# Decoder block on one core: three products in column quarters, the bias moved to the residual, two DMAs for four, and new places

## The chip, the cores and the metric

The kernel runs on one core of a Trainium2 chip. A core has five engines, each with an in-order queue: TensorE (PE; its weight loads are listed as PEld), VectorE (DVE), ScalarE (ACT), GpSimd (POOL) and SyncE (SP), which here issues nearly all DMA transfers. The metric is the device time of one execution in microseconds (us).

## The reference

For 128 sequences of 64 rows with 128 features (8192 rows) the reference computes three sublayers, each followed by a residual addition and a layer norm:

```python
x = _layernorm(x + _L0_attn_ref(x, ...))           # linear attention, 16 heads of 64, 32 exp features
x = _layernorm(x + _L0_xattn_ref(x, ctx_1024, ...))  # softmax attention, 16 heads of 8
x = _layernorm(x + _L0_ffn_ref(x, ...))            # ternary weights, 128 -> 512 -> 128, gelu, inner layer norm
```

The linear attention takes `q' = exp(q wq_feat)`, `k' = exp(k wk_feat)`, divides `q' (k'^T v)` by `q' . sum(k') + 1e-6`, and projects with `Wproj` plus a bias. The softmax attention scales scores by 1/sqrt(8). The feed-forward part replaces both weight matrices by signs, with zeros for small entries, takes the exact gelu, normalises the 512 hidden values of a row with weight and bias, and projects back. Everything is fp32.

## The kernel before

The rows are cut into 16 groups of 512 rows: 8 sequences, or four *row tiles* of 128 rows. For each group a fixed list of steps is made; a step is a Python closure that issues its instructions on several engines. Nothing is scheduled by a compiler: `PLACE` gives each step a number, group g adds `g * ROUND` (44) and a shift from `SHIFT` (one of three dictionaries, by the first letter of the step's name, indexed by group), one-time preparations have their numbers in `PREP`, all steps are sorted, and their instructions are issued in that order. So the order on each engine's queue is the order of these numbers. A step of the second and third sublayers is placed one round later than its group (`r = g + 1`), and its number may exceed 44 by much, so that in one round PE works on the linear attention of group g, the softmax attention of group g-1 and the feed-forward part of groups g-2 and g-3.

The steps of a group are these (t counts row tiles, b sequences, c blocks of 128 of the 512 features):

- `lx`, `lc`, `lg`: loads of x transposed, the context transposed, and x; `lxs`, `lgs`, `xs` split such a tile into an fp32r high part (ACT) and the rest (POOL or DVE). A product of two split operands is three fp32r matmuls (`product3`, L427 to L429).
- `K0-3`, `Q0-3`: projections to features and their exp on ACT (kp, qp). `ks`, `kT`: the sums of k'. `G0-3`: k'^T x by sequence, in the 64-row shape (L530), copied out to gT by DVE (0, 3) or ACT (1, 2). `D`, `dT`: the denominators and their reciprocals as a table dT, `E0-3`: their spread over features (L582), multiplied into qp on DVE. `M0-7`: gT times the folded matrix U by sequence (L596), copied out to m by ACT, two sequences at a time. `Y0-3`: the output, x1 = bias product (L610) + qp m (L615) + x, with statistics on DVE; `Yn`: the norm.
- `xk`, `xq`: the projections of the softmax attention, each cut into three bf16 pieces (`pieces`), which six DMAs each copy into interleaved rows of `krep` and `qrep`. `xv`: the values (L659), copied by ACT into the block tile vbd. `xt`: four transposes of x1 (L670). `X0-3`: scores once, only for their row maxima on DVE (L700). `xm`: the maxima transposed (L705), negated and written as two bf16 pieces, mn, which go by DMA into two spare rows of each half of `qrep` (L712). `S0-3`: scores again, now with the maxima subtracted, and exp to pt on ACT (L728). `P0-7`: pt times values (L744). `C0-1`: division and transposition on DVE. `O0-1`: the output projection (L771) plus xb (`xr`: x1 plus bias, on POOL), statistics; `xn`: the norm on ACT.
- `ft`: transposes of x2 (L792). `fb`: the bias added to x2 on POOL. `fw0-1`: the first product (L807, L808) and gelu on ACT to gf. `fs0-1`: squares of gf on ACT to sk, summed on POOL to sq. `fo0-1`: the last product (L833, 130 columns: 128 outputs, and two for the mean) and the mean of the squares (L834, one column). `fv`: mean and variance, rstd on POOL; `fx`: scale and residual, statistics, on DVE; `fn`: the norm on ACT and the DMA out.

PE's array is used in several shapes, given by `tile_position`. Full width is one 128x128 weight tile. In a *column quarter* the weights are 128x32, four such products stand side by side, and each writes 32 partitions of the result. ks, D, M, Y and P are quarters; G uses two halves of 64 rows; X and S use 64x64 quadrants; the rest is full width. An fp32 matmul is two instructions in the profile, an fp32r matmul one.

PSUM has two double banks (`two()`: G, fw, M, X, S) and four single banks (`one()`: all others). A buffer comes free when its reader has copied it out, so an engine that reads late keeps PE from starting a later step.

Of the kernel before, what the change touches and what calls it, by code (L numbers as in the profile page):

```python
# [55 lines left out]
)  # L56
BIG = 5
# [27 lines left out]
def decoder_block(  # L85
# [347 lines left out]
    def shift(g, place):  # L433
        return SHIFT[2 if place[0] == "f" else 1 if place[0] in "xXSPCO" else 0].get(g, 0)
# [191 lines left out]
    def pieces(step, ps, bias, roles, rep):  # L626
# [7 lines left out]
        for i, part in enumerate(roles):  # L634
            nc.sync.dma_start(out=rep[i::HD], in_=pc[:, part, :])
# [339 lines left out]
```

## Time and profile before

| | us |
|---|---|
| median of 3 runs (lowest to highest) | 739.92 (739.57 to 741.57) |
| the profiled execution's own time | 740.87 |
| its span, first to last instruction | 738.9 |
| PE busy | 687.4 |
| DVE busy | 572.9 |
| ACT busy | 504.3 |
| POOL busy | 323.4 |
| rstd of the four layer norms and the inner one on POOL (L385, 64 of them) | 66.0 |
| PE waiting for POOL's sum of squares (once) | 5.1 |
| PE waiting for DVE's copies of gT (12 times) | 4.3 |
| PE waiting for the DMA of the maxima (3 times) | 2.3 |

How to read it: a line of the timeline gives the start, the duration, the engine, the line of the program, the operation, what it writes and reads, and how many instructions were merged; in brackets stands the idle time just before, and what ended it. Matmuls overlap in the array, and their listed durations include the way through it; the cost of one inside a full stream is the distance between starts. The granted clock (PEclk) is the TensorE clock as a share of full speed.

### The profile page before, as it was taken

The page shows a single profiled execution, that of the slowest core. Times are in us where ns is not written, and L with a number is a line of the kernel's source. Part 1 is how long each engine was busy: PE and PEld are TensorE (multiplying, and loading weights), DVE is VectorE, ACT ScalarE, POOL GpSimd, SP SyncE. Part 2 cuts the span into 40 slices and gives each one's busy share as a digit, 9 for nine tenths or more (in the row PEclk, how much of TensorE's full clock was granted, in tenths as well). Part 3 has the DMA queues.
Part 4 walks back from the last instruction along what each step waited for, and adds up shares of the span by engine and source line. Part 5 has one row for each costly group of instructions (what it writes and reads, how often), then busy time and mean ns, then how long its engine had stood idle before and what let it go on. Part 6 is the DMA issues. An engine that isn't in the chain of part 4 may idle for free.

```text
span 738.9 us, 36655 instructions
## 1 busy us (share of the span) xinstructions
PE 687.4 (93%) x16551; PEld 576.9 (78%) x16551; DVE 572.9 (78%) x1379; ACT 504.3 (68%) x757; POOL 323.4 (44%) x383
## 2 busy tenths in 40 slices
PE   6989999999999999999999999999999999976753
PEld 5767878787878888887878788887888787865653
DVE  1568898797879797988879787979889796958532
ACT  2636565867688687877686886878686877654750
POOL 4744414263553626263634526262635445143451
PEclk9989999999999999999999999999999999996875
DMA  7005131302122131413032221314131312203000
GB/s 191 3 31 136 43 106 31 102 24 77 55 75 75 49 101 34 117 34 92 31 84 65 76 75 47 103 34 116 35 80 42 82 53 52 71 24 82 19 23 20
DMA packets 58428, 47.82 MB, mean 65 GB/s; under 512 B 7952, under 2 KB 54032, under 8 KB 58272
## 3 DMA queue, kind: packets, MB, share of 16 engines
q1 hardware_dynamic: 57632, 45.37, 22.6%
q8 instruction: 129, 2.11, 1.2%
q0 software_dynamic: 320, 0.08, 0.2%
q14 instruction: 27, 0.22, 0.1%
q10 hardware_dynamic: 320, 0.03, 0.0%
HBM read 15.58 MB, written 4.19 MB: 27 GB/s over the span
## 4 chain that ended last, share of the span: by engine, by line
PE 68%; DVE 18%; POOL 4%; ACT 4%; DMA 2%; issue 2%; SPq 1%; POOLq 0%; ACTq 0%; DVEq 0%
PE two L596 13%; PE one L833 8%; PE one L615 8%; PE one L427 6%; PE one L428 4%; PE one L429 4%; PE two L530 3%; DVE bns L390 3%; PE two L697 3%; POOL rstd L385 2%; PE one L517 2%; DVE x L851 2%; PE one L610 2%; DVE gT L395 2%; PE one L582 2%
## 5 line engine op out<-in xcount | busy, mean ns | idle before, releaser
L596 PE MATMUL two<-U,gT 128*32 128x128 f32 x4096 | 123.4, 275 | 0.8 <-DVE mx L700 0.5
L596 PEld LDWEIGHTS two<-U,gT 128*32 128x32 f32 x4096 | 112.0, 111 | 1.8 <-DVE mx L700 0.6
L397 ACT COPY m<-two 128x1024 f32<-128x1024 f32 x64 | 64.9, 1013 | 30.3 <-PE two L596 30.1
L399 POOL TENSOR_SCALAR khl<-kp 128x512 fp32r<-128x512 f32 x32 | 20.2, 631 | 137.6 <-ACT kp L496 137.6
L833 PE MATMUL one<-w2c,gf 128*128 128x130 f32 x512 | 78.1, 301 | 1.5 <-ACT gf L810 1.5
L700 DVE TENSOR_REDUCE mx<-two 128x16 f32<-128x1024 f32 x64 | 74.9, 1213 | 3.3 <-PE two L697 3.3
L833 PEld LDWEIGHTS one<-w2c,gf 128*128 128x128 f32 x512 | 71.4, 210 | 4.8 <-ACT gf L810 2.1
L410 POOL TENSOR_TENSOR sq<-sk 128x512 f32<-128x512 f32 x16 | 20.8, 1299 | 116.9 <-ACT sk L816 116.9
L385 POOL TENSOR_TENSOR rstd<-veps,mhalf 128x4 f32<-128x4 f32 x64 | 66.0, 1032 | 5.3
L615 PE MATMUL one<-m,qp 128*32 128x128 f32 x2048 | 68.1, 273 | 0.0
L383 POOL TENSOR_SCALAR veps<-mv 128x4 f32<-128x4 f32 x64 | 15.4, 240 | 116.2 <-DVE mv L844 73.8
L423 ACT ACTIVATE x<-x,nm,rstd 128x128 f32<-128x128 f32 x128 | 51.3, 482 | 20.6 <-DVE nm L422 20.6
L728 ACT ACTIVATE pt<-two 128x1024 f32<-128x1024 f32 x64 | 62.7, 1021 | 1.9 <-PE two L725 1.7
L390 DVE BATCH_NORM_STATS2 bns<-x 128x6 f32<-128x128 f32 x192 | 55.5, 289 | 5.5
L615 PEld LDWEIGHTS one<-m,qp 128*32 128x32 f32 x2048 | 57.4, 110 | 0.2 <-issue 0.2
L508 ACT ACTIVATE qp<-one,bqk 128x512 f32<-128x512 f32 x64 | 43.7, 684 | 16.3 <-PE one L429 12.0
L496 ACT ACTIVATE kp<-one 128x512 f32<-128x512 f32 x64 | 38.3, 598 | 22.0 <-PE one L429 13.5
L530 PE MATMUL two<-khl,xgh 64*128 64x512 f32 x256 | 49.0, 418 | 4.6 <-DVE gT L395 4.3
L707 ACT ACTIVATE mn<-one 64x128 bf16<-64x128 f32 x16 | 4.3, 270 | 70.1 <-PE one L705 70.1
L744 PE MATMUL one<-pt,vbd 128*32 128x64 f32 x2048 | 46.7, 224 | 0.5 <-DVE x L851 0.5
L410 POOL TENSOR_TENSOR sq<-sq,sk 128x512 f32<-128x512 f32 x32 | 40.9, 1280 | 6.1 <-ACT sk L816 4.8
L842 DVE COPY mv<-one 128x2 f32<-128x2 f32 x32 | 4.9, 154 | 49.4 <-PE one L834 49.4
(217 smaller groups left out, 1812.6 us busy)
## 6 DMA issues: line engine op xcount, KB each, us to landing
krep<-pc SPq DMA_DIRECT2D x96, 128.0 KB, 2.4
qrep<-pc SPq DMA_DIRECT2D x96, 128.0 KB, 3.0
xT<-in_x_T_dram SPq DMA_DIRECT2D x16, 256.0 KB, 3.1
xg<-in_x_dram SPq DMA_DIRECT2D x16, 256.0 KB, 3.1
cT<-in_ctx_T_dram SPq DMA_DIRECT2D x16, 256.0 KB, 3.3
out_dram<-x SPq DMA_DIRECT2D x16, 256.0 KB, 2.4
qrep<-mn SPq DMA_DIRECT2D x64, 8.0 KB, 1.8
wTk<-in_L_attn_Wk_T_dram SPq DMA_DIRECT2D x1, 512.0 KB, 4.4
```

The lines of the kernel that those rows point to most:

```text
L385: nc.gpsimd.tensor_tensor(r, v, mhalf, ALU.pow)
L390: nc.vector.bn_stats(s, src)
L397: nc.scalar.copy(dst, src)
L410: eng.tensor_tensor(dst, a, b, op)
L423: nc.scalar.activation(x[:, t, :], x[:, t, :], AF.Identity, scale=r[:, t : t + 1], bias=nm[:, t : t + 1])
L530: nc.tensor.matmul(gps[:, b, :], lhsT=xp[r, t, :], rhs=z.khl[t // 2][r, kp, t % 2, :], start=(i == 0), stop=(i == 2), tile_position=(64 * ...
L596: nc.tensor.matmul(z.mps[b // 2][32 * j : 32 * j + 32, b % 2, c * D : c * D + D], lhsT=z.gT[b // 4][:, b % 4, h * F : h * F + F], rhs=w.U[ ...
L615: nc.tensor.matmul(yps[32 * i : 32 * i + 32, 0:D], lhsT=z.qp[:, c, t * P + 32 * i : t * P + 32 * i + 32], rhs=z.m[q // 4][:, q % 4, c, :], ...
L700: nc.vector.tensor_reduce(z.mx[:, :, :, t], sps.rearrange("p h (c k) -> p h c k", k=S), AX.X, ALU.max)
L728: nc.scalar.activation(z.pt[t].rearrange("p h b c q -> p (h b c q)"), sps.rearrange("p h n -> p (h n)"), AF.Exp, scale=HD ** -0.5)
L744: nc.tensor.matmul(z.cps[i // 4][32 * c : 32 * c + 32].rearrange("p (n k q) -> p n k q", k=2, q=32)[:, q // 32 : q // 32 + 2, k, :], lhsT= ...
L833: nc.tensor.matmul(ps[:, o : o + WF], lhsT=z.gf[c // 2][:, c % 2, n], rhs=w.w2c[:, c, :], start=(c == 0), stop=(c == NFC - 1))
```

## The change

Seven things are changed; what is computed stays the same.

1. `Y`: the bias product is no longer the first of the matmuls that add up in a tile of Y. A new step `W` computes it for all four row tiles of the group into one bank, at full width and in fp32r, and DVE adds the bank to xg, the residual.
2. `O`: each of the four output products of a group (two in each of two steps) becomes four products with 32 columns of weights.
3. `xv`: so do the four products of the values.
4. `fo`: so do the sixteen products of the last feed-forward matrix, and the mean of squares. For the last group alone, the two tiles of squares get separate buffers, and PE adds up the four parts instead of POOL.
5. `xm`: the maxima go to `qrep` in two DMAs of 64 rows in place of four of 32.
6. `pieces`: the six DMAs go out sorted by piece.
7. `PREP`, `SHIFT` and `PLACE` get new numbers, so the order of steps changes everywhere.

```diff
 PREP = {
...
+    "lb": -167.2995, "lk": -149.8596, "lc2": -141.5964, "c1": -137.7757, "lq": -112.8302, "lv": -47.1274,
+    "fk": -39.9216, "x0": -37.5866, "c0": -32.4310, "wb": -31.6615, "fq": -25.4067, "bqk": -11.7754, "U0": -11.4537,
+    "c2": -9.5186, "U1": -6.7768, "x1": -3.4930, "WB": 6.0100, "E": 8.5443, "x2": 17.9416, "c3": 18.6377,
+    "end": 19.6009, "w0": 45.9851, "w1": 82.4437, "w2": 93.0686, "w3": 128.7876,
...
+        @at(g, "W")
+        def _():
+            ps = one()
+            for t in range(GT):
+                n = slice(t * P, t * P + P)
+                nc.tensor.matmul(ps[:, n], lhsT=z.dT[:, n], rhs=w.WB, start=True, stop=True)
+            nc.vector.tensor_tensor(z.xg.rearrange("p t d -> p (t d)"), ps, z.xg.rearrange("p t d -> p (t d)"), ALU.add)
...
             yps = one()
-            for i in range(4):
-                n = slice(t * P + 32 * i, t * P + 32 * i + 32)
-                nc.tensor.matmul(yps[32 * i : 32 * i + 32, 0:D], lhsT=z.dT[:, n].bitcast(FP), rhs=w.WB.bitcast(FP), start=True,
-                                 stop=False, tile_position=(0, 32 * i))
...
-        for i, part in enumerate(roles):
+        for part, i in sorted((part, i) for i, part in enumerate(roles)):
             nc.sync.dma_start(out=rep[i::HD], in_=pc[:, part, :])
...
             for i in range(2):
-                for h in range(2):
-                    o = 64 * h + R2 - 2 + i
-                    nc.sync.dma_start(out=qrep[o : o + 1], in_=mn[32 * h : 32 * h + 32, i, :])
+                nc.sync.dma_start(out=qrep[R2 - 2 + i :: R2], in_=mn[:, i, :])
...
             for i in range(2):
-                nc.tensor.matmul(ps[:, i * D : i * D + D], lhsT=z.cnT[k][:, i, :], rhs=w.cwo, start=True, stop=True)
+                for j in range(4):
+                    r = slice(32 * j, 32 * j + 32)
+                    nc.tensor.matmul(ps[r, i * D : i * D + D], lhsT=z.cnT[k][:, i, r], rhs=w.cwo, start=True, stop=True,
+                                     tile_position=(0, 32 * j))
...
-            s = later.f1.tile([P, 2, GN], FP, tag="sk", name="sk")
+            s = later.f1.tile([P, 2, GN], FP, tag="sk1" if k and g == NG - 1 else "sk", name="sk")
             nc.scalar.activation(s.rearrange("p i n -> p (i n)"), z.gf[k].rearrange("p i n -> p (i n)"), AF.Square)
-            if k == 0:
+            if g == NG - 1:
+                z.sk[k] = s
+            elif k == 0:
...
                 for c in range(NFC):
-                    nc.tensor.matmul(ps[:, o : o + WF], lhsT=z.gf[c // 2][:, c % 2, n], rhs=w.w2c[:, c, :], start=(c == 0), stop=(c == NFC - 1))
-                nc.tensor.matmul(ps[:, o + WF : o + WF + 1], lhsT=z.sq[:, n], rhs=rff, start=True, stop=True)
+                    for j in range(4):
+                        q = slice(32 * j, 32 * j + 32)
+                        nc.tensor.matmul(ps[q, o : o + WF], lhsT=z.gf[c // 2][:, c % 2, n][:, q], rhs=w.w2c[:, c, :],
+                                         start=(c == 0), stop=(c == NFC - 1), tile_position=(0, 32 * j))
+                for j in range(4):
+                    q = slice(32 * j, 32 * j + 32)
+                    sq = [z.sk[c // 2][:, c % 2, n] for c in range(NFC)] if g == NG - 1 else [z.sq[:, n]]
+                    for c, s in enumerate(sq):
+                        nc.tensor.matmul(ps[q, o + WF : o + WF + 1], lhsT=s[:, q], rhs=rff, start=(c == 0),
+                                         stop=(c == len(sq) - 1), tile_position=(0, 32 * j))
```

The tables of numbers are best read as the order that they give. One round in the middle, step and group, before:

```
K0.9 xq.7 fw0.5 D2.8 P5.6 M0.8 dT.8 P7.6 M1.8 M4.8 M5.8 fs0.5 M2.8 M3.8 C1.6 O0.6 fw1.5 E2.8 K1.9 E1.8 xv.7 lc.8
X0.7 X1.7 K2.9 E0.8 lx.10 ks0.9 xs.8 ks1.9 M6.8 M7.8 E3.8 K3.9 lgs.9 O1.6 X2.7 X3.7 Y0.8 Y2.8 ks2.9 Y1.8 fs1.5 Y3.8
ks3.9 xm.7 Q0.9 fn.4 Q1.9 xn.6 Q3.9 lg.10 fo0.5 kT.9 xr.7 S0.7 S1.7 Q2.9 Yn.8 fo1.5 fv.5 ft.6 lxs.10 fb.6
P0.7 P1.7 S2.7 P2.7 P3.7 S3.7 fx.5 xk.8 G0.9 G1.9 D0.9 D1.9 P4.7 D3.9 P6.7 C0.7 xt.8 G2.9 G3.9
```

and after:

```
K0.9 xv.7 fs1.5 M4.8 O0.6 M5.8 M2.8 O1.6 lx.10 M3.8 E0.8 K1.9 X0.7 X1.7 E3.8 lc.8 E1.8 K2.9 ks0.9 fn.4
M6.8 M7.8 ks1.9 X2.7 E2.8 K3.9 lg.9 W.8 X3.7 ks2.9 Y0.8 Y1.8 fb.5 Y2.8 Y3.8 ks3.9 xm.7 kT.9 xs.8 Q0.9 Q3.9 Q2.9
xn.6 fo0.5 S0.7 Yn.8 S1.7 fo1.5 fv.5 lgs.9 ft.6 S2.7 P0.7 fx.5 P2.7 P3.7 P1.7 S3.7 Q1.9 xk.8 G0.9 xt.8 G1.9
P4.7 xr.7 C0.7 D0.9 D3.9 lxs.10 G2.9 G3.9 xq.8 fw0.6 P5.7 P6.7 P7.7 fs0.6 C1.7 D2.9 D1.9 M0.9 M1.9 fw1.6 dT.9
```

The start before: `lk c0 lb lc2 fk bqk c1 lq lx.0 lg.0 lxs.0 fq K0.0 lv x0 K1.0 K2.0 lx.1 ks0.0 lgs.0 ks1.0 K3.0 U0 ks2.0 ks3.0 U1 Q0.0 Q1.0 Q3.0 lg.1 kT.0 x1 E Q2.0 lxs.1 G0.0 G1.0 D0.0 D1.0 D3.0 wb G2.0 G3.0 K0.1 c2 D2.0 M0.0 dT.0 M1.0 M4.0 x2 M5.0 M2.0 M3.0 WB E2.0`; after: `lb lk lc2 c1 lq lx.0 lv fk x0 lxs.0 c0 wb fq K0.0 lx.1 K1.0 K2.0 ks0.0 ks1.0 K3.0 lg.0 bqk ks2.0 U0 c2 ks3.0 kT.0 U1 Q0.0 Q3.0 Q2.0 x1 lgs.0 Q1.0 WB G0.0 G1.0 E D0.0 D3.0 lxs.1 G2.0 G3.0 D2.0 D1.0 M0.0 x2 M1.0 c3 dT.0 end K0.1 M4.0 M5.0 M2.0 lx.2 M3.0 E0.0`.

More of the change, by code (lines that the diff above doesn't have):

```diff
@@ L433, in shift @@
     def shift(g, place):
-        return SHIFT[2 if place[0] == "f" else 1 if place[0] in "xXSPCO" else 0].get(g, 0)
+        return SHIFT[2 if place[0] == "f" else 1 if place[0] in "xXSPCO" else 0].get(g, 0) + EDGE.get(g, {}).get(place, 0)
     def at(g, place):
@@ L658, in _ @@
             for t in range(GT):
-                nc.tensor.matmul(ps[:, t * P : t * P + P], lhsT=z.cT[:, t * P : t * P + P],
-                                 rhs=w.cwvT.rearrange("p o c h e -> p (o c h e)"), start=True, stop=True)
+                for j in range(4):
+                    r = slice(32 * j, 32 * j + 32)
+                    nc.tensor.matmul(ps[r, t * P : t * P + P], lhsT=z.cT[:, t * P : t * P + P][:, r],
+                                     rhs=w.cwvT.rearrange("p o c h e -> p (o c h e)"), start=True, stop=True,
+                                     tile_position=(0, 32 * j))
             v5 = ps.rearrange("p (t o n e) -> p t o n e", t=GT, o=2, e=HD)
@@ L832, in _ @@
                 for c in range(NFC):
[L833 to L834 removed]
+                    for j in range(4):
+                        q = slice(32 * j, 32 * j + 32)
+                        nc.tensor.matmul(ps[q, o : o + WF], lhsT=z.gf[c // 2][:, c % 2, n][:, q], rhs=w.w2c[:, c, :],
+                                         start=(c == 0), stop=(c == NFC - 1), tile_position=(0, 32 * j))
+                for j in range(4):
+                    q = slice(32 * j, 32 * j + 32)
[3 more added lines that the diff above has]
+                                         stop=(c == len(sq) - 1), tile_position=(0, 32 * j))
         @at(r, "fv")
@@ L920, in _ @@
                                 ALU.subtract)
-    groups = [SimpleNamespace(pt={}, kp={}, khl={}, cps={}, cnT={}, mps={}, gT={}, m={}, gf={}, fps={}) for _ in range(NG)]
+    groups = [SimpleNamespace(pt={}, kp={}, khl={}, cps={}, cnT={}, mps={}, gT={}, m={}, gf={}, sk={}, fps={}) for _ in range(NG)]
     for g in range(NG):
```

5 lines of the change are left out of this document (4 added, 1 removed), and 42 rows, old and new, of tables (PLACE, PREP, SHIFT).

## The prediction

> **What bounds the kernel now.** I read the page first (busy shares, then the slices), then the times by windows, the waits of TensorE (PE), and last the timeline of one middle round and of the end. Page and windows:
>
> ```profile
> PE 687.4 (93%) x16551; PEld 576.9 (78%) x16551; DVE 572.9 (78%) x1379; ACT 504.3 (68%) x757; POOL 323.4 (44%) x383
> ...
> PEclk9989999999999999999999999999999999996875
> ...
> 40.00:60.00 20.00, 17.31 (x286) 13.86 (x285) 12.55 (x30) 6.37 (x11) 7.53 (x10) 0.83 0.16 50
> 160.00:640.00 480.00, 474.61 (x11998) 400.41 (x11987) 404.28 (x979) 364.85 (x546) 218.69 (x233) 1.00 0.25 68
> ...
> 700.00:720.00 20.00, 12.02 (x64) 10.41 (x64) 8.99 (x34) 9.88 (x18) 11.30 (x12) 0.76 0.05 15
> 720.00:739.00 19.00, 6.84 (x32) 6.76 (x32) 4.08 (x19) 1.65 (x4) 2.54 (x5) 0.59 0.09 26
> ```
>
> Columns of a window: length, then busy time of PE, PEld, DVE, ACT, POOL; PEclk; DMA share; GB/s. The reader should see two regimes. From 160 to 640 us PE is busy 474.6 of 480 us at full clock: a round (one group of 512 rows) costs what PE's instruction stream costs, 40.8 us (the transposes of the maxima stand at 365.23, 406.07, 446.76, 487.55). Before 60 and after 640 us PE waits, and its clock drops to 0.83 and 0.59.
>
> Inside a busy PE the matmul durations overlap, so costs are read from start to start. The timeline of a middle round:
>
> ```profile
> 396.27 0.40 PE L582 MATMUL one<-dT,E 128*128 128x512 f32 x1
> 396.60 0.64 PE L517 MATMUL one<-kp,ksel 128*32 128x128 f32 x16
> ...
> 399.95 0.60 PE L771 MATMUL one<-cwo,cnT 128*128 128x128 f32 x4
> 400.48 0.71 PE L697 MATMUL two<-krep,qrep 62*64 62x64 bf16 x64
> 401.12 0.42 PE L610 MATMUL one<-WB,dT 128*32 128x128 f32 x8
> 401.37 1.06 PE L615 MATMUL one<-m,qp 128*32 128x128 f32 x32
> 402.24 0.40 PE L517 MATMUL one<-kp,ksel 128*32 128x128 f32 x8
> ...
> 407.61 1.06 PE L833 MATMUL one<-w2c,gf 128*128 128x130 f32 x8
> 408.50 0.28 PE L834 MATMUL one<-rff,sq 128*128 128x1 f32 x2
> ...
> 420.44 0.66 PE L670 MATMUL one<-ident,x 128*128 128x128 f32 x4
> 421.48 0.50 PE L530 MATMUL two<-khl,xgh 64*128 64x512 f32 x2 [0.38 <-DVE gT L395]
> ```
>
> Three readings. Quarter products cost (402.24-401.37)/32 = 27.2 ns each, 109 ns for the four of a full width; L833 at full width costs (408.50-407.61)/8 = 111 ns: **quarters alone save nothing**. A change of array shape costs: L582 takes 0.33 us ahead of a quarter step, 0.23 between its like, and the first full-width matmul after another shape takes 0.34. So about 0.10 us to leave a shape, another 0.11 to enter full width, 0.09 to enter the 64-row shape of G, 0.02 to enter the others. And the one regular wait is 0.38 us at the third G for a copy of gT.
>
> **The change part by part (steady round).**
> *Bias.* L610 goes: 0.24 + 3 x 0.22 = -0.90 us. W puts four 128-wide fp32r matmuls of 128 columns in its place. Nearest rows: transposes of the same shape, L670 and L792, 0.46 us for 4; below, L834 (same weights, one column) 70 ns, so 0.28; above, L427's 512 columns, 0.23 each, so 0.93. I take 0.46: size and type agree. W stands right behind K3, so it adds no change of shape. On DVE it adds one 128x512 add, 0.675 us (row L583). DVE is busy 404.3/480 x 40.8 = 34.4 us a round, so 35.1 after. Queued behind it are the maxima of X3 and the adds of Y. I lay the new order out with the costs above: Y0 wants the last product with E (E2) at 25.6 us after the round's xk, DVE, which does E2 ahead of W, gives it at 25.2. Hidden, with 0.4 to spare; without that cover it costs its 0.68.
> *Last feed-forward product.* A pair of row tiles now takes 2.15 us (407.61 to 409.76). In quarters: 2 x 32 x 27.2 ns x 130/128 = 1.77, and 2 x 8 one-column quarters at 13.8 ns (L744: 16 in 0.22) = 0.22: 1.99. Two pairs: -0.32. If a one-column quarter cost as much as a 128-column one (27.2), +0.11.
> [...]
> *Output.* L771: 4 in 0.36 us among full-width neighbours, twice; in quarters 16 x 27.2 = 0.435: +0.15. *Values.* L659: 0.99 less 0.10 for the change of shape, 0.89; in quarters 0.87: 0.
> *New places: shapes.* I sorted the steps of one round by their places and counted neighbours on PE of unlike shape: 22 before, 27 after, of which the two at xm's sides are alike in both. The others by kind: into full width 0.21 each, 7 and 8; into G 0.19, 2 and 3; the rest 0.12, 11 and 14. That is 3.17 and 3.93: +0.76. Each unquartered fp32 product also leaves its successor 0.09 slower (the L427 behind L834 takes 0.32); three such places vanish: -0.27.
> *New places: waits.* 0.37 at G2 and 0.15 between K0 and xq (424.00-423.62 is 0.38 for a 0.23 step) can go. In the new order G1 lies between the transposes and G2, so G2 has 0.3 us of slack; but G3 then waits for ACT's copy of G1, ready 0.15 ahead of it, and X1 for the copy of M2M3, ready about 0.2 late. I leave 0.25 of the 0.52: -0.27. SP: lx, lc, lg and the out-transfer keep one place each per round; sorting the parts of qrep puts three transfers ahead that need no later piece; between xq and X0 lie 12.3 us (before 11.5), against 0.7 + 6 x 0.78 + 3.0 us for the pieces. xr (1.28 us on POOL) now comes ahead of C0, 11 us before O0 reads it; fb (1.29, POOL) comes a round later than its ft, still 8 us before fx. xgl, behind rstd on POOL, is ready 0.8 us ahead of G0.
> *Round:* -0.90+0.46-0.32+0.15+0.76-0.27-0.27 = **-0.39**; bounds: no waits left and W at 0.28: -0.8; W at 0.93, one-column quarters at 27.2, waits as before: +0.8. Fourteen rounds: **-5.5** (-11 to +11).
>
> **Start.** Between 40 and 51 us PE waits 1.43 us (for dT, whose cast took 3.48 instead of 0.43 while POOL filled qrep), then 1.26 (nhalf of WB), and runs until 51 at half clock, where 64 quarters take 3.26 us instead of 1.86. The new order has WB and the memsets of wb and c2 long before; krep's cast (2.29) and qrep's memset (3.5) still precede dT. I expect E0 at 41.6 instead of 42.1 and no second wait: 0.5 + 1.3 + 1.2 of slow clock = **-3** (-5.5 if the clock stays up, 0 if dT is as late).
>
> **End.** Two DMAs of maxima for four: issuing four takes 2.8 us. In the middle they are hidden (4.6 us of PE work from xm to S0), worth nothing. At 653.9, where no later group fills the gap, PE waits 1.69 + 0.41 us for them; two issues of 0.70 less: **-1.4** (0 to -2). The last group's sum of squares:
>
> ```profile
> 714.30 0.71 PE L833 MATMUL one<-w2c,gf 128*128 128x130 f32 x4 [1.29 <-ACT gf L810]
> 720.08 0.59 PE L834 MATMUL one<-rff,sq 128*128 128x1 f32 x2 [5.07 <-POOL sq L410]
> 720.53 2.08 PE L833 MATMUL one<-w2c,gf 128*128 128x130 f32 x8
> ...
> 716.30 1.06 ACT L816 ACTIVATE sk<-gf 128x1024 f32<-128x1024 f32 x1 [2.05 <-POOL sq L410]
> 717.43 2.60 POOL L410 TENSOR_TENSOR sq<-sq,sk 128x512 f32<-128x512 f32 x2 [1.17 <-ACT sk L816]
> ```
>
> PE waits 5.07 us for squares that ACT could not start (their tile was still read by POOL) and POOL then summed, and goes on at half clock (1.87 us for 8 instead of 0.89), to 726.93. After the change the second square has its own tile: ready at 714.24 + 1.06 = 715.3, no POOL. PE goes on at 714.3 with half a row tile (0.44) and three whole ones (0.88 each, as above), and for each of the four tiles 32 one-column quarters, since the four parts are now summed on PE (32 x 13.8 ns = 0.44): 4.8 us at full clock, 9.7 at half, so it ends at 719.1 to 724.0. I take the middle, rounded: **-5** (-2.9 to -7.8). What is late next is the gelu, then fv and fx as before.
>
> *Sum:* -5.5-3-1.4-5 = -14.9 on the profiled execution's 740.87 (span 738.9 and 1.97 around it): 726.0. That execution lies 0.95 above the median of 739.92: **725**.
>
> **The rivals.** *ACT becomes the bound at X1 (slower).* From fw0 to M3 the new order gives ACT two table loads (1.28 each), two gelus (1.02), two squares (1.06), kp and khl (0.60, 0.59), four copies to vbd (1.58) and three of m (1.01) before X1's buffer is free: 12.5 us, about 11.8 from start to start (a copy of 1.01 is followed after 0.91, 430.28 to 431.19), against 11.9 of PE work, where before vbd and a square stood elsewhere. For: no margin. Against: ACT is busy 364.9 of 480 us. Every us late is paid in each of 14 rounds; with the rest as forecast, the result is slower beyond (14.9+2.2)/14 = 1.2 us a round; at 1.5 the time is 725 + 21 = 746. Chance 0.12.
> *The shapes eat it.* Waits stay at 0.52 or W costs 0.93: the round gains 0 and the ends give 9.4: 730.5. For: five more changes are certain. Band 730 to 737.7, chance 0.25.
> *All waits go:* -0.82 x 14, start -5.5, end -9.8: 713. Band below 720, chance 0.14.
> *The change does nothing that counts:* W at 0.93 and one-column quarters at 27.2 give +0.5 x 14 = +7, the ends 9: 738. Within 0.3% (2.2 us, what a measurement of this kernel can tell from nothing), chance 0.10.
> The forecast, 720 to 730: 0.39.
>
> **How the numbers follow.** Faster: 0.39 + 0.25 + 0.14 = 0.78; same 0.10; slower 0.12. Range 714 to 742: from the case with no waits to the edge of the slower case, leaving out that case and a little below. The forecast's own range is 720 to 730.
>
> **What would show it.** W's four matmuls at about 0.46 us from start to start; L610 gone; 27 changes of shape a round; period 40.4. The third G without its wait for gT. In the end no wait of PE for POOL's sq, and the last one-column products less than 10 us after the last gelu. In the start no wait behind WB. Wrong it would be with a period of 41 or more, and waits of X for ACT's copies of m, or of G for gT.

## The result and the profile after

The changed kernel takes 763.29 us (median of 4 executions, 759.06 to 767.73) against 740.75 of the kernel before, measured beside it: a ratio of 1.0304, 95% interval 1.0235 to 1.0374. It is 3% slower. The forecast was 725, the range 714 to 742: wrong in sign and outside the range.

The profiled execution, the fastest of the four, took 759.06 us, its span 757.3. From the page of the changed kernel come PE's busy time (and the other engines'), the granted clock by slices, and the queue that brings instructions (packets, MB, share):

```profile
PE 679.5 (90%) x18887; PEld 557.5 (74%) x18887; DVE 570.8 (75%) x1395; ACT 505.8 (67%) x757; POOL 324.2 (43%) x380
...
PEclk9999999999999999999999999999999999999796
...
q8 instruction: 148, 2.42, 1.3%
```

PE has 2336 more pairs of weight load and matmul than before, and is busy for 8 us less. The instruction queue brings 148 packets of 16 KB; it was 129. This line matters below. The windows of the changed kernel:

```profile
40.00:60.00 20.00, 16.68 (x396) 14.13 (x388) 14.99 (x24) 7.72 (x11) 9.67 (x8) 0.91 0.23 68
160.00:640.00 480.00, 451.42 (x13024) 372.68 (x13024) 383.96 (x939) 346.55 (x521) 212.85 (x223) 1.00 0.24 64
700.00:720.00 20.00, 14.74 (x555) 12.62 (x556) 11.43 (x33) 11.75 (x18) 7.05 (x9) 0.74 0.07 19
```

Between 160 and 640 us PE was busy 474.6 of 480 us; now 451.4. A regime in which PE's own stream sets the time has become one in which PE stands still, at full clock. PE's waits in that window (total, times, longest):

```profile
PE two L705 <- ACT m L397: 16.2, 20, 1.4
PE two L731 <- issue: 3.2, 4, 1.4
PE one L846 <- issue: 2.8, 6, 0.7
PE one L750 <- issue: 2.3, 4, 0.8
PE one L620 <- issue: 2.0, 4, 0.7
PE one L427 <- DVE x L870: 1.8, 1, 1.8
```

So there are two losses: X (the maxima's products) waits for ACT's copies of m, and several steps wait for "issue", that is, for nothing that another engine does. The first is best seen at X3, in the timeline of one round (start, duration, engine, step; in brackets the idle time before it and what ended it):

```profile
373.53 1.93 PE L596 MATMUL two<-U,gT 128*32 128x128 f32 x64
...
374.27 0.59 ACT L404 ACTIVATE khl<-one 128x512 fp32r<-128x512 f32 x1
...
374.90 1.31 DVE L410 TENSOR_TENSOR khl<-kp,khl 128x512 fp32r<-128x512 f32 x1 [0.17 <-ACT khl L404]
...
376.13 0.15 DVE L422 SCALAR_TENSOR_TENSOR nm<-mv,rstd 128x4 f32<-128x4 f32 x1
...
376.31 1.65 ACT L423 ACTIVATE x<-x,nm,rstd 128x128 f32<-128x128 f32 x4 [1.45 <-DVE nm L422]
...
377.02 0.56 PE L608 MATMUL one<-WB,dT 128*128 128x128 f32 x4
...
377.87 0.99 ACT L397 COPY m<-two 128x1024 f32<-128x1024 f32 x1
...
378.91 0.45 PE L705 MATMUL two<-krep,qrep 62*64 62x64 bf16 x32 [1.33 <-ACT m L397]
```

Read it from the bottom. X3 waits 1.33 us for the PSUM tile that ACT empties at 377.87. M6 and M7, the products into that tile, ran on PE from 373.53 to 375.46. ACT was idle then: from 374.86 it stood for 1.45 us in front of the *final norms* of an older group (fn, L423), which wait for nm, a DVE step of 0.15 us, which itself stood behind the khl subtraction of 1.31 us. ACT's queue is in order, so the copy stood behind a step that nobody needed soon.

The second loss, a stalled stretch of the changed kernel. These are PE's rows only:

```profile
387.69 0.71 PE L731 MATMUL two<-qrep,krep 64*64 64x64 bf16 x64
388.33 0.63 PE L846 MATMUL one<-w2c,gf 128*32 128x130 f32 x10
389.68 0.76 PE L846 MATMUL one<-w2c,gf 128*32 128x130 f32 x19 [0.72 <-issue]
...
392.43 0.54 PE L750 MATMUL one<-pt,vbd 128*32 128x64 f32 x22
393.42 0.83 PE L750 MATMUL one<-pt,vbd 128*32 128x64 f32 x42 [0.46 <-issue]
```

PE stops in the middle of a step, after 10 of 32 pairs and after 22 of 64, though the profile shows nothing that they wait for, and the two stops end 3.74 us apart. (The counts are pairs of a weight load and a matmul; an fp32 product is two.) The instruction queue in the same kernel, from 387.25 to 387.50 and from 390.75 to 391.00 us:

```profile
q8 instruction: 1, 0.02, 23.9%
q8 instruction: 1, 0.02, 30.6%
```

So a packet of instructions starts 2.3 to 2.6 us ahead of the end of each stop. It is not these two alone: all 16 stops for issue of more than 0.3 us between 160 and 640 us end 2.2 to 2.7 us behind the start of such a packet.

To set these in proportion I put every middle round (200 to 600 us) into a ledger, from start to start: what each product costs among its like, what changes of shape cost by the prices of the prediction, and the rest, which holds the waits.

| kernel | period us | own time | shapes (number) | rest |
|---|---|---|---|---|
| before | 40.82 | 36.27 | 3.53 (22.2) | 0.97 |
| after | 43.16 | 35.70 | 4.21 (26.9) | 3.28 |

Of the 3.28, X3 is 1.29 and X1 0.49 (from start to start, so a little more than PE's idle time there); the stops for issue are 0.93 (10.3 us in the 11.1 rounds of the window); the remaining 0.57 is of the kind that before had too.

### The profile page after: what moved, and what is told of

It is laid out like the page before. It is cut to its first block, busy times and chain, and to the rows that moved or that the text cites. A ratio compares the mean times of both kernels' runs of the same rounds, so it can differ in the third digit from the quotient of the medians.

```text
span 757.3 us, 41375 instructions
## 1 busy us (share of the span) xinstructions
PE 679.5 (90%) x18887; PEld 557.5 (74%) x18887; DVE 570.8 (75%) x1395; ACT 505.8 (67%) x757; POOL 324.2 (43%) x380
## 4 chain that ended last, share of the span: by engine, by line
PE 61%; DVE 14%; ACT 13%; issue 6%; POOL 3%; DMA 2%; POOLq 0%; ACTq 0%; DVEq 0%
PE one L846 8%; PE two L596 7%; PE two L530 7%; PE one L620 6%; PE one L427 4%; PE one L750 4%; PE one L429 3%; PE one L428 3%; PE two L731 3%; ACT x L423 3%; DVE mx L708 2%; ACT m L397 2%; PE one L556 2%; PE two L816 2%; PE two L817 2%
## 5 line engine op out<-in xcount | busy, mean ns | idle before, releaser
L596 PE MATMUL two<-U,gT 128*32 128x128 f32 x4096 | 128.0, 273 | 0.6 <-issue 0.4
L708 DVE TENSOR_REDUCE mx<-two 128x16 f32<-128x1024 f32 x64 | 76.7, 1221 | 13.2 <-PE two L705 13.1
L423 ACT ACTIVATE x<-x,nm,rstd 128x128 f32<-128x128 f32 x128 | 52.6, 482 | 38.1 <-DVE nm L422 38.1
L846 PE MATMUL one<-w2c,gf 128*32 128x130 f32 x2048 | 72.0, 284 | 4.5 <-issue 3.0
L397 ACT COPY m<-two 128x1024 f32<-128x1024 f32 x64 | 63.1, 1008 | 10.8 <-PE two L596 10.4
L410 POOL TENSOR_TENSOR sq<-sq,sk 128x512 f32<-128x512 f32 x30 | 38.4, 1279 | 68.8 <-ACT sk L825 67.6
L846 PEld LDWEIGHTS one<-w2c,gf 128*32 128x32 f32 x2048 | 56.6, 113 | 12.8 <-issue 5.1
L620 PE MATMUL one<-m,qp 128*32 128x128 f32 x2048 | 60.4, 273 | 2.0 <-issue 2.0
L530 PE MATMUL two<-khl,xgh 64*128 64x512 f32 x256 | 53.4, 434 | 0.0
L705 PE MATMUL two<-krep,qrep 62*64 62x64 bf16 x2048 | 28.2, 197 | 21.0 <-ACT m L397 16.5
L705 PEld LDWEIGHTS <-qrep 62*64 62x64 bf16 x2048 | 23.0, 110 | 31.5 <-issue 30.4
```

Source lines behind the costliest of these rows:

```text
L397: nc.scalar.copy(dst, src)
L423: nc.scalar.activation(x[:, t, :], x[:, t, :], AF.Identity, scale=r[:, t : t + 1], bias=nm[:, t : t + 1])
L530: nc.tensor.matmul(gps[:, b, :], lhsT=xp[r, t, :], rhs=z.khl[t // 2][r, kp, t % 2, :], start=(i == 0), stop=(i == 2), tile_position=(64 * ...
L596: nc.tensor.matmul(z.mps[b // 2][32 * j : 32 * j + 32, b % 2, c * D : c * D + D], lhsT=z.gT[b // 4][:, b % 4, h * F : h * F + F], rhs=w.U[ ...
L620: nc.tensor.matmul(yps[32 * i : 32 * i + 32, 0:D], lhsT=z.qp[:, c, t * P + 32 * i : t * P + 32 * i + 32], rhs=z.m[q // 4][:, q % 4, c, :], ...
L705: nc.tensor.matmul(sps[64 * b : 64 * b + 64, h, c * S : c * S + S], lhsT=qrep[64 * h : 64 * h + R2 - 2, c, n], rhs=krep[64 * h : 64 * h + ...
```

## The experiments

Times are medians; each ratio is to the kernel before run beside it, with its 95% interval.

### The final norms behind M7

```
-    ... "fx": 134.2681, "fn": 162.0740,
+    ... "fx": 134.2681, "fn": 163.2500,
```

> The changed kernel with one place altered: the norm fn (162.07 to 163.25) comes behind M7, so on ACT the copy of M6M7 goes ahead of fn's four norms. Theory A (ACT's order): in the changed kernel X3 waited 1.34 us in most rounds for that copy (the fn norms were themselves 1.45 us late behind DVE); the wait at X3 goes, 1.0 to 1.3 us in each of 13 rounds, 13 to 17 us in all: about 748 us; the wait at X1 (0.45) stays. Theory B (PE's instructions come too late): 1 to 2 us at most, the waits named issue stay at about 10 us between 160 and 640 us. Theory C (the add of the bias on DVE or the 27 changes of shape are the cost): no more than 2 us.

Measured: 745.68 us, 1.0075 [1.0044, 1.0106]; 17.6 less than after. Period 41.65. In ACT's rows of its timeline the copy is now ahead of the norms, and X3 does not wait:

```profile
366.64 0.60 ACT L496 ACTIVATE kp<-one 128x512 f32<-128x512 f32 x1 [1.78 <-PE one L517]
367.13 0.59 ACT L404 ACTIVATE khl<-one 128x512 fp32r<-128x512 f32 x1
368.39 1.01 ACT L397 COPY m<-two 128x1024 f32<-128x1024 f32 x1 [0.66 <-PE two L596]
369.30 1.65 ACT L423 ACTIVATE x<-x,nm,rstd 128x128 f32<-128x128 f32 x4
```

The waits for ACT's m fall from 16.2 to 3.5 us; those for issue stay (9.3). One place number, which changes the order on ACT and leaves that of DVE's steps there as it was, is worth 2.3% of the kernel. This cause is shown.

### The last feed-forward product at full width

```
+                if g < NG - 1:
+                    for c in range(NFC):
+                        nc.tensor.matmul(ps[:, o : o + WF], lhsT=z.gf[c // 2][:, c % 2, n], rhs=w.w2c[:, c, :], ...)
+                    nc.tensor.matmul(ps[:, o + WF : o + WF + 1], lhsT=z.sq[:, n], rhs=rff, start=True, stop=True)
+                    continue
```

> The changed kernel with the last feed-forward product back at full width in all groups but the last; places unchanged. Theory B (the quarters of this product raise PE's instructions so far that their supply stalls): PE's waits named issue between 160 and 640 us fall from 10.4 us to under 2. The product costs 0.4 us a round more and 0.24 less for shapes, so 5 to 11 us faster: about 755 us. If those waits are something else they stay, and the kernel is within 3 us of the changed one or slower. Theory A: the waits at X1 and X3 stay as they are (16 us).

Measured: 752.59 us, 1.0177 [1.0146, 1.0209]; 10.7 less than after, though the same products then take 0.3 us a round more of PE. PE's waits from 160 to 640 us in that kernel:

```profile
PE two L705 <- ACT m L397: 15.2, 20, 1.3
PE one L620 <- issue: 2.1, 3, 1.4
PE one L779 <- issue: 0.6, 1, 0.6
```

The stops for issue fall from 10.3 to 2.9 us, the waits for ACT stay. The two losses are separate.

### Old code under the new places, new code under the old ones

The first has before's code with after's PREP, SHIFT and PLACE; the second after's code with before's numbers and one more for the new step:

```
+    "W": 27.9000,
```

> The kernel before with the new numbers of places, and none of the other edits. Theory A: the waits of X1 and X3 for ACT's copies of m appear here too (12 us or more between 160 and 640 us), no waits named issue; full-width O between the quarters of M adds 0.66 us a round: 760 to 775 us. If the edits themselves are the cost, the time is 738 to 748.

> All the edits with the old numbers of places, W put behind K3. Theory A alone: no waits for copies of m, and the round gains 0.2 us, the end 6: 728 to 734 us. Theory A and B: the supply of instructions still stalls, 5 to 12 us in all: 735 to 745. Theory C: 755 or more, as slow as the changed kernel.

Measured: 787.84 us, 1.0643 [1.0620, 1.0666], for the places alone, more than the 760 to 775 expected; 748.03 us, 1.0099 [1.0067, 1.0130], for the edits alone, between two of the readings (735 to 745, and 755 or more). With the old code the new order has the wait of X for ACT's m too (16.2 us in the window), so this wait comes from the order, not from the quarters. The new order also costs before's code 11 us of start (the first transposition of the maxima at 97.3 instead of 86.0). The edits alone slow the kernel as well: own time falls to 35.73 as it should, but there are 29.6 changes of shape (4.63 us), and the rest grows to 1.81; in it are stops for issue of 3.9 us in the window (10.3 in the changed kernel). Neither part is the gain that the other hides.

### The edits under the old places, rounds at full width

The lines show what changes against the edits alone:

```
-                for j in range(4):
-                    r = slice(32 * j, 32 * j + 32)
-                    nc.tensor.matmul(ps[r, i * D : i * D + D], lhsT=z.cnT[k][:, i, r], rhs=w.cwo, ...)
+                nc.tensor.matmul(ps[:, i * D : i * D + D], lhsT=z.cnT[k][:, i, :], rhs=w.cwo, start=True, stop=True)
...
```

> The edits under the numbers of before (PREP, SHIFT, PLACE), with the output, values' and last feed-forward product left at full width except that of the last group; what stays of the change is the bias product as four full tiles added to the residual, the last group's squares read without POOL's sums, and the two DMAs of maxima. Earlier run with all the edits under those numbers: 748.0 us, period 42.15 us, of it 4.63 switches and 1.81 excess. If the quarters cost what they add in shape switches and in instruction supply (both theories' common ground, and supply's in particular), the period falls to base 35.8 + switches 3.6 + excess 0.9 = 40.3 and the time is 727 to 733 us: faster than before, and the end alone is 6 us shorter. If the quarters are harmless and it is the bias product that does not fit under those numbers (one more tile of PSUM, one more DVE addition), the time stays at 744 to 750.

Measured: 742.22 us, 1.0020 [1.0004, 1.0037]. Neither branch: 5.8 us less than with the quarters, not the 15 to 21 expected. Period 41.58: own time is 36.01 (35.8 expected) and shapes are 3.54 (3.6), but the rest is 2.09 where I had 0.9. PE's waits name little of it: the third G's for gT (4.2 us in the window, as in before) and O's for DVE's product with E (2.0 us, 0.17 a round). The bias step, put there by hand, is 0.26 us a round cheaper in own time and about 1.1 dearer in the rest. Where most of the 1.1 lies is open, and another place for the step was not tried.

### Both causes taken away, and a third place moved

The first kernel has the two edits above together. The second also has ACT's second square behind M3, because X1 waited behind it:

```
-    ... "fs1": 109.1483,
+    ... "fs1": 112.3000,
```

> After, with the final norms placed behind M7 and the last feed-forward product at full width in all groups but the last: both causes found taken away at once. Alone they gave -17.6 and -10.7 us. If they are two separate causes (ACT's queue at X3; supply of instructions in the dense stretch), they add up: 763.3 - 28.3 = 735 us, from 732 to 738. If they are one stall seen from two sides, the pair gives little more than the larger: 743 to 746.

> The run with the final norms moved and the last feed-forward product at full width, and besides ACT's second square of the feed-forward moved behind M3, so that the copy of m1 that X1 waits for (0.49 us a round in the changed kernel) is ahead of it. If that square is what holds the copy up, the wait goes: 7 us less than the run beside it, about 728 us. If only the place of the wait moves (the square then delays the copy for X2, or POOL's sums and with them the last feed-forward product), the time is that of the run beside it, within 3 us, or longer.

Measured: 737.39 us, 0.9938 [0.9916, 0.9959], and 746.95, 1.0080 [1.0050, 1.0109]. The first is within 2.4 us of the sum of the two single gains: two separate causes. Its ledger is 36.04 + 4.03 + 0.81, for a period of 40.93 (the parts are summed over slightly fewer records): with the waits gone the round costs what the products and shapes cost, and that is before's 40.82 within about 0.1. So even the mended rounds gain nothing: by the profiled executions the start is 3.1 us longer than before, the 14 rounds are 2.8 longer, and the end is 12.4 shorter. The second shows how little room ACT has: X's wait for m vanished, but PE now waits 5.2 us for ACT's kp and 4.3 for DVE's qp, and the end, with the last group's square later, is 6.9 us longer.

### One-column products six times over

The final norms stand behind M7 here too.

```
-                for j in range(4):
+                for j in [0, 1, 2, 3] * (6 if g < NG - 1 else 1):
                     q = slice(32 * j, 32 * j + 32)
                     sq = [z.sk[c // 2][:, c % 2, n] ...
```

> After with the final norms behind M7 (745.7 us, period 41.65), and each one-column product of the last feed-forward step issued six times over instead of once, into the same place with the same operands: 80 more pairs of weight load and matmul in a round of the 14, and nothing else. By their measured time on PE (7 ns a pair) that is 0.56 us a round, 8 us in all: 752 to 756. If the supply of instructions is the limit in this stretch, each pair costs what a packet of 128 pairs takes when they come without pause (3.5 us, so 27 ns): 2.2 us a round, 30 us in all: 770 to 780. A value between says what part of the added instructions falls where the supply had slack.

Measured: 813.05 us, 1.0954 [1.0905, 1.1003]; period 45.91, 4.26 more. That lies above both numbers, and the cause is my count: each of these products goes out as *two* pairs (8 records for four quarters in the trace of after), so 160 pairs a round were added, 320 instructions, not 160. The run's page of the profile confirms it: 46175 instructions against 41375 (2400 pairs in 15 groups), 19 packets more, 253 instructions a packet. Put right, the readings are 1.4 to 1.8 us a round for the pairs' own 9 to 11 ns (48 in 0.52 us) and 160 x 27.3 ns = 4.4 us for the supply. 4.26 was measured. The rows add up to about as much: PE's stops for issue are 33.0 us in the window, 3.2 a round, against 9.3 and 0.8 with the norms moved alone, and the pairs' own time comes on top. In PE's rows of this run the pairs flow at 11 ns each (403.44 to 403.96 for 48), and then PE stops:

```profile
403.44 0.58 PE L852 MATMUL one<-rff,sq 128*32 128x1 f32 x48
...
406.65 0.31 PE L846 MATMUL one<-w2c,gf 128*32 128x130 f32 x3 [0.97 <-issue]
...
410.39 0.28 PE L852 MATMUL one<-rff,sq 128*32 128x1 f32 x6 [1.70 <-issue]
```

The queues of the same run from 400 to 416.5 us (packets, MB, share) show five packets of instructions:

```profile
q8 instruction: 5, 0.08, 2.1%
```

To within 0.25 us those packets start at 400.5, 404.0, 407.75, 411.5 and 415.0: 3.5 to 3.75 us apart, and the stops end 3.74 us apart, as in the changed kernel, each some 2.6 us behind the start of a packet. (From 410 to 416 us this round runs at a granted clock of 0.50; in the whole window the mean is 0.99, so the clock is a small part of the 4.26.) About 250 instructions are 125 pairs of weight load and matmul, and 3.5 us over 125 pairs is an estimate of some 28 ns for each where PE stops for packets. That is the supply theory, with its number: the stops follow the packets, and they come and go with the number of instructions (33.0 us of stops in the window here, 9.3 without the added pairs, 2.9 with the last product at full width).

### The same products elsewhere

The run with the final norms moved, with 80 one-column products (160 pairs) a round added in 14 rounds: first as two blocks of 40, ahead of Q1 and xk, then as four blocks of 20, ahead of G1, G2, xq and fw0.

```
+            for j in [0, 1, 2, 3] * (10 if 0 < g < NG - 1 else 0):
+                nc.tensor.matmul(ps[32 * j : 32 * j + 32, 0:1], lhsT=ident[:, 32 * j : 32 * j + 32], rhs=rff, start=True,
+                                 stop=True, tile_position=(0, 32 * j))
```

> After with the final norms behind M7, and the same number of added one-column products as in the run that issued them six times over (80 in a round), but placed among the 128x512 products, 40 ahead of the second product of the queries and 40 ahead of the product of the cross keys, in 14 rounds. The added ones count twice over in the trace of that run (48 records for 24 products): 160 pairs, so 320 instructions or 1.25 packets a round, which at 3.5 us a packet is 4.4 us a round, and 4.26 was measured. If packets are short only where the products are short, the wide stretch has room for these (it uses about a third of the supply) and they cost their own 9 to 11 ns each and two shape switches: 1.7 to 2.0 us a round, 769 to 775 us. If an added pair costs 27 ns wherever it stands, the time is that of the other run less one round: 804 to 812.

> Where the run with two blocks of 40 put its products, PE had just come out of the dense stretch and stood still for packets in the first block; this one spreads the same 80 (160 pairs) as four blocks of 20 ahead of the second and the third G, of the product of the cross queries and of the first feed-forward product, 3 to 9 us into the wide stretch. If packets are fetched ahead there while PE consumes slowly, the cost is the pairs' own 9 to 11 ns and four changes of shape there and back (0.2 to 0.25 us each): 2.3 to 2.8 us a round over the run with the final norms behind M7 (745.7), 778 to 785 us, and no PE idling for issue there. If an added pair costs 27 ns wherever it stands (and the clock is halved after such a stall, as it was in the run with two blocks), 4.4 to 6 us a round: 808 to 831.

Measured: 831.23 us, 1.1230 [1.1204, 1.1256], and 776.61, 1.0475 [1.0439, 1.0512]. The first was a surprise, above either reading (period 48.05). Its PE rows, and its windows of the dense stretch and of what follows, say why:

```profile
433.19 0.24 PE L508 MATMUL one<-rff,ident 128*32 128x1 f32 x6
435.19 0.79 PE L508 MATMUL one<-rff,ident 128*32 128x1 f32 x74 [1.77 <-issue]
435.91 0.70 PE L427 MATMUL one<-xTh,wqh 128*128 128x512 f32 x1
436.40 0.63 PE L428 MATMUL one<-xTl,wqh 128*128 128x512 f32 x1
436.83 0.63 PE L429 MATMUL one<-xTh,wql 128*128 128x512 f32 x1
```

```profile
423.30:433.00 9.70, 9.36 (x362) 8.21 (x361) 5.34 (x21) 7.54 (x14) 3.10 (x5) 1.00 0.04 11
435.90:443.00 7.10, 6.74 (x104) 4.39 (x96) 1.30 (x2) 1.99 (x3) 1.14 (x2) 0.52 0.04 10
```

The two blocks stand directly behind the dense stretch: PE gets through 6 of 80 pairs and stops for 1.77 us. Behind that stop the granted clock is 0.52 for 7 us though PE is busy (6.74 of 7.10), and the 128x512 products follow each other in 0.43 us instead of 0.23. PE's stops for issue are 27.3 us in the window, 2.7 a round against 0.8; with the pairs' own 1.4 to 1.8 that is 3.3 to 3.7 of the 6.4 us a round. The halved clock is the likely rest: the mean from 160 to 640 us is 0.93, which is some 7 us at half clock a round. Here the clock is 0.52 behind stops of 0.34 and 1.77 us; behind the 1.33 us waits of X3 in the changed kernel it did not fall (1.00 in 160 to 640). Whether the stops alone bring it about, or the one-column products beside them as well, is not separated here.

The second run, three to nine microseconds further on, gave 1.97 us a round: four blocks at 0.44 us (402.23 to 402.67 for 40 pairs) are 1.76, and the rest is shapes. No block stops for issue; the other stops are no longer than without the blocks (7.9 us in the window against 9.3). The same number of products thus costs 4.26 us in the dense stretch, 6.4 behind it and 1.97 among wide products. In these runs supply limits only in and just behind a stretch where short products stand close together.

### The ends alone, and with the last group's quarters

Before's code and places; first with the last group's squares unsummed, the maxima in two DMAs and the sorted parts; then, besides, the last group's product and squares in quarters.

```
+            if g == NG - 1:
+                z.sk[k] = s
...
-                for h in range(2):
-                    o = 64 * h + R2 - 2 + i
-                    nc.sync.dma_start(out=qrep[o : o + 1], in_=mn[32 * h : 32 * h + 32, i, :])
+                nc.sync.dma_start(out=qrep[R2 - 2 + i :: R2], in_=mn[:, i, :])
```

> The kernel before with the ends of the change alone: the last group's squares multiplied without POOL's sums, the maxima in two DMAs, the pieces' DMAs in order of their part; no tile split, no step moved, no bias step. The prediction gave -5 us for the last squares and -1.4 us for the maxima; the stretch from the last maxima's transposition to the end became 6.0 us shorter in the changed kernel. So 734 to 735.5 us if the end's gain stands by itself; 738 to 741 if the end only became shorter because of what comes before it.

> The kernel before with the ends of the change, as in the run of the ends alone (735.6 us), and the last group's last feed-forward product and its sums of squares in quarters too, the other groups at full width. At full width eight one-column products of the squares take 1.57 us there from start to start, at half clock, four times over; in the changed kernel 32 quarters take 0.6 to 1.0 us. If that carries to the end: 2 to 3 us less, 732.5 to 734. If the end waits for what DVE and ACT do behind the products, nothing: 735 to 736.

Measured: 735.56 us, 0.9939 [0.9920, 0.9959], and 733.46, 0.9888 [0.9865, 0.9912]: the second is the fastest kernel of this study, 1.1% faster than before. Its period is before's (40.81). The end itself, from the second last transposition of the maxima, is 89.1 us before, 84.5 with the ends and 80.5 with the quarters too. PE's rows of the two ends, first at full width:

```profile
713.33 1.71 PE L836 MATMUL one<-rff,sk 128*128 128x1 f32 x8
714.90 2.08 PE L833 MATMUL one<-w2c,gf 128*128 128x130 f32 x8
```

and in quarters:

```profile
712.55 1.15 PE L841 MATMUL one<-rff,sk 128*32 128x1 f32 x29
713.51 0.44 PE L836 MATMUL one<-w2c,gf 128*32 128x130 f32 x3
```

For one row tile the eight at full width take 1.57 us from start to start, 0.2 each; 29 of the 32 quarters that replace them take 0.96, both at half clock. Here quarters are worth having: PE stops nowhere for issue in this end, and the end waits for PE. Part of the 4.0 us is the clock: from 714.9 to 721.7 us it is 1.00 with the quarters and 0.50 at full width, where PE is busy all the time.

### The new order at full width, and with the old setup

Both start from the kernel with the two causes taken away; the first has output and values at full width, by the edit shown for the old places, the second before's PREP:

```
-    "lb": -167.2995, "lk": -149.8596, ...
+    "lk": -303.4064, "c0": -263.0074, ...
```

> The run with the final norms moved and the last feed-forward product at full width (737.4 us, period 40.93: base 36.04, switches 4.03, excess 0.81), and the output and the values' products at full width too. By the ledger the base grows by 0.15 and 2.9 shape switches go (-0.3 to -0.5): period 40.6 to 40.8, 732 to 735.5 us. If the quarters of these two are what lets their neighbours run on without a switch under the new order, the time is 738 to 742.

> The run with the final norms moved and the last feed-forward product at full width, with the setup's places (PREP) of before. The first maxima's transposition came at 89.2 us there and at 86.0 us before. If the setup's order is what lost these 3.1 us, it comes at 85.5 to 86.5 and the time is 733 to 735; if it is the groups' own new places that make the start longer, it stays near 89 and the time at 736 to 739.

Measured: 737.97 us, 0.9982 [0.9960, 1.0004], with output and values at full width too; 755.33, 1.0208 [1.0188, 1.0229], with the old setup. In the first the period is the same (40.96 against 40.93): 28.3 changes of shape instead of 25.2, as these steps stand between quarters in the new order, and a smaller rest (0.42). So in a round the quarters of the output and of the values are worth nothing either way; that the whole kernel takes 0.9982 and not 0.9938 comes from a start and an end that are each 2 us longer, and why was not found. The second refutes my guess about the setup: the old PREP under the new places puts the first transposition at 104.0 us instead of 89.2. The start is a matter of both sets of numbers; which single one costs the 3 us no run shows (a candidate stands below, under *Start*).

## Why the prediction was wrong

By the profiled executions the forecast span was 724.0, and 757.3 came: 33.3 us. By stretches, parted at the first and the second last transposition of the maxima (86.04 and 649.78 before, 90.41 and 677.92 after):

| stretch | predicted | measured | missed by |
|---|---|---|---|
| start | -3 | +4.4 | 7.4 |
| 14 rounds | -5.5 | +23.8 | 29.3 |
| end | -6.4 | -9.8 | -3.4 |

*Bias, last feed-forward product, output, values:* right in the sum. Together they were to take 0.61 us from a round's own time (0.90 - 0.46 + 0.32 - 0.15), and it fell by 0.57. W's four products start 0.48 us before what follows (369.88 to 370.36 in the run with the norms moved), against 0.46. A pair of row tiles takes 2.02 us with the shape change behind it, against 1.99. A one-column quarter is two pairs of 7 ns each (8 pairs in 0.05 to 0.06 us), half of the 13.8 that I took for a pair. By parts the ledger is less sure than in the sum: under the old places it gives the bias step 0.26, where the rows give 0.42 (0.90 less 0.48).

*Shapes:* right, 26.9 of them against 27, +0.68 us against +0.76.

*Waits (the step that failed):* "I leave 0.25 of the 0.52". The rest of the ledger went from 0.97 to 3.28. I followed the transfers, POOL's steps and G's and X1's buffers through the new order, and at X1 I was near ("ready about 0.2 late": 0.49). I did not follow ACT's queue to X3, where the final norms stand ahead of the copy of m and themselves wait for a DVE step of 0.15 us. That is 1.29 us a round; moving the one step brought 17.6 us. The third G's wait for gT did go, as forecast; and the prediction's own sign of being wrong, a period of 41 or more with waits of X for ACT's copies of m, is what came (43.16).

*A term that was missing:* I priced a quarter by PE's time from start to start, and the instructions at nothing. Before, the two halves of the last feed-forward product, the scores and the second product of the cross attention are parted by six 128x512 products of the queries (409.76 and 411.28 in the prediction's round): 242 pairs from 407.61 to 416.71, 38 ns each. After, the queries stand ahead of all this, and 356 pairs come in a row, 428.43 to 435.58 where nothing stops: 20 ns each, against the estimate of about 28 from the packets. Taking the quarters out is worth 8.3 us with the norms moved and 10.7 without. A packet more comes with 248 more instructions by the pages of before and of the changed kernel (4720 in 19 packets), and with 253 in the run six times over. In the changed kernel PE's stops for issue in the steps of this stretch (L731, L846, L750) are 8.3 us in the window from 160 to 640 us; before, the list of PE's waits there has 0.4 for issue.

*Start:* "krep's cast (2.29) and qrep's memset (3.5) still precede dT. I expect E0 at 41.6". E0 came at 48.98. The second wait did go. But "still" is a misreading: before, the cast of krep stood on DVE *behind* dT, as these rows of before's timeline show:

```profile
41.60 0.43 DVE L395 CAST dT<-dt 128x512 fp32r<-128x512 f32 x1
42.13 2.29 DVE L370 CAST krep<-last 128x4096 bf16<-128x4096 f32 x1
```

The new places put it ahead of dT, and there it lies beside POOL's memsets of qrep and vbd. In the changed kernel:

```profile
38.90 3.51 POOL L371 MEMSET qrep<- 128x4096 bf16 x1
40.14 5.42 DVE L370 CAST krep<-last 128x4096 bf16<-128x4096 f32 x1
45.48 0.70 DVE L565 STREAM_TRANSPOSE dd<-one 128x512 f32<-128x512 f32 x1
...
48.98 0.50 PE L582 MATMUL one<-dT,E 128*128 128x512 f32 x1 [3.32 <-DVE dT L395]
```

The cast takes 5.42 us instead of 2.29, and dT's steps queue behind it on DVE. That is as long as if it had stood still until 43.27 and then taken its 2.29; POOL's next memset, of vbd, ended at 43.41. The prediction had the sign: the cast of before that it gives as 3.48 us and puts down to the same memset (its line, L571, takes 0.23 us in the changed kernel; the 0.43 us that it is held against is another cast, dT's). It struck that price out where the memset no longer met it, and did not ask what the memset meets now. PE's wait of 3.3 us for dT stands in the run with both causes taken away too, and is as long as what that run's start loses against before (3.1); that the one is the other is likely, but no run moved this cast alone.

*End:* right in kind, and 3.4 us more than forecast. PE's wait for POOL's sq at the last group is gone; the last PE product comes 67.1 us after the second last transposition, before 77.2. With the old order the ends bring 4.6 us and the quarters of the last group 4.0 more, part of that by the clock.

*The rivals:* "ACT becomes the bound at X1 (slower)" was nearest: the same engine, tile and sign, at 0.12. Its place was wrong, and so was its kind: ACT was not too busy, it stood in line. It gave 746, and 763.29 came; that the kernel takes 745.7 with ACT's order mended is chance, since what is left there is the second cause, which no rival had. A chance of 0.78 for faster rested on a ledger of one engine.

## What to carry to other kernels

When steps move, follow every in-order queue through one whole round of the new order, also those of engines that are idle a quarter of the time (ACT here, busy 346.6 of 480 us): at each step that frees a PSUM tile, ask what stands ahead of it and what *that* waits for. Price small products twice, by PE's time and by instructions: where pairs stand closer than the packets brought them here (some 28 ns, by the estimate above), splitting a product fourfold cost stops for issue (10.3 us in the window with the last product in quarters, 2.9 at full width), and 160 pairs a round cost 1.97 us among wide products where they cost 4.26 in the dense stretch. Splits paid where PE did not stop for issue and the end waited for it, as in the last group here (4.0 us, part of it by the clock).

## What was not expected of the hardware

- Instructions came at a rate: packets of about 250 came 3.5 to 3.75 us apart where PE stopped for them (to within 0.25 us; 3.3 at the closest in before and in the changed kernel), and the stops ended 2.2 to 2.7 us behind the start of one (all 44 of more than 0.3 us, in the changed kernel and in the run six times over). How much lies ahead in store is not shown; six pairs into a block behind the dense stretch PE stopped for 1.77 us.
- Stops of 0.34 and 1.77 us within 4 us were followed by 7 us at a granted clock of 0.52 with PE busy (6.74 of 7.10 us). In the end with the last products at full width the clock is 0.50 from 713.3 to 720.0 us though PE's rows fill all of these 6.70 us; one-column products take nearly half of them.
- A one-column product on a quarter is two pairs at 7 to 11 ns; at full width such a pair takes 70 ns (L834 in before), and 196 in the end, at half clock. In the last group, where the eight pairs of one quarter follow each other, it is 20 ns at full clock (29 in 0.58) and 33 at half (29 in 0.96), not the 13.8 of the prediction.
- A cast on DVE beside a memset on POOL took 5.42 us instead of 2.29; another, of 128x128, took 3.48 in before, beside the memset of qrep, and 0.23 in the changed kernel.
